# First attention: products of weights and values in eight 64-row tiles over two PSUM banks

## The chip, the cores and the metric

The kernel runs on one core of a Trainium2 chip. The metric is the device time of one execution in microseconds (us). Three runs of the kernel before took 1479.85, 1480.92 and 1483.95 us; their median is 1480.92.

The names of the engines are those of the profile: PE is TensorE (matmuls), PEld the loading of weights into TensorE (it runs beside PE), DVE is VectorE, ACT ScalarE, POOL GpSimd, and SP the engine that issues most DMAs. PSUM, where matmuls put their results, has eight banks; one bank holds a tile of 128 partitions by 512 fp32 numbers.

## The reference

The program is one layer stack over a sequence of 1024 tokens of width 512: a first attention, a feed-forward part with experts, a second attention with 4-bit weights, and the same feed-forward part again, each behind a layer norm and with a residual. The change lies in the first attention alone:

```
q = hidden_state @ wq + bq      # 32 heads of 16
k = hidden_state @ wk + bk      # 8 groups of 16, each shared by 4 heads
v = hidden_state @ wv + bv
scores = jnp.einsum('bhqd,bhkd->bhqk', q, k) * scale
probs = jax.nn.softmax(scores, axis=-1)
out = jnp.einsum('bhqk,bhkd->bhqd', probs, v)
out = jnp.swapaxes(out, -1, -2).reshape(B, -1, HEAD_DIM * NUM_HEADS)
return out @ wo + bo
```

There is no mask: each of the 32 heads weighs all 1024 keys for all 1024 queries.

## The kernel before

The first attention works on pairs of heads, 16 of them (`PAIRS`). For each pair it goes through the keys in eight tiles of 128 (`kt`, `NT` = 8). One turn of that inner loop (lines 530 to 561) is called a step here; there are 128 steps.

Queries and keys are split into a high and a low part and stacked, so that a score matmul contracts 64 rows. The stacks fill rows 0 to 63 (`low`) and 64 to 127 (`high`), with the same content, so two 64-row matmuls can run side by side, one on each half of the array. `side_by_side` (L396) takes matmuls from two lists in turn, one for each half. I call such a couple a slot. A step issues:

- Scores for a later pair, up to four or five of 128 queries by 512 keys (`half_score`, matmul L337, into a tile `sc` of a pool of three banks). DVE takes the largest of each row straight from PSUM (L346). These maxima are needed before the exponentials of that pair.
- Exponentials of the present pair (`exponentials`), four for each step, u = 0 to 3 (two heads by two halves of the queries). Each is two matmuls into one bank `st`: keys by queries (L378), and a second one that subtracts the maxima (L386). ACT then writes exp of the bank to `pT` (L390). In the high list stand u = 0, 1 and 3, in the low list u = 2 behind three scores.
- The products of the step before (`weighted(*behind)`): for each u a matmul of `v_sb` (128 keys by 32 columns: 16 values and 16 ones, which give the sum of the weights) with `pT[:, u]` into rows 32u to 32u + 31 of the one bank `po` (L411). The four column tiles share the array. These matmuls are fp32, and each shows as two records, one for each pass. The bank gathers over the eight steps of a pair.

After the last key tile DVE copies `po` to `oT` (L420). At kt = 3 of the next pair `tail` transposes `oT` on PE into a bank `pt` and DVE divides by the sums (L431 to L436). At even kt `place_largest` transposes the maxima of a later pair, if they are complete, into a bank `mp` (L360); ACT copies it (L362) and DMAs place it. Every fourth pair `project_out` multiplies by the output weights into a bank `py` (L451).

The eight PSUM banks are dealt out at lines 248 to 250: three to `sc`, four to the pool `st_ps`, one to `po`. The pool `st_ps` serves `st`, but also `mp`, `pt`, `py` and the banks of the stages ahead of and behind the loop. A tile takes a bank that has been read out; where none is free, its first matmul waits.

The order on PE in this loop is the order of the program text (`manual_schedule`, L502), so a matmul that waits holds back everything behind it on PE. The order on the other engines is set by the framework's scheduler.

Of the kernel before, what the change touches and what calls it, by code (L numbers as in the profile page):

```python
# [11 lines left out]
F32 = mybir.dt.float32  # L12
# [4 lines left out]
ALU = mybir.AluOpType  # L17
AX = mybir.AxisListType
PSUM = bass.MemoryType.PSUM

P = 128
S = 1024
C = 512
NC_ = C // P
NT = S // P
# [16 lines left out]
def kernel(  # L42
# [28 lines left out]
    nc = tc.nc  # L71

    def pool(stack, name, bufs=1, space=None):
        kw = {} if space is None else {"space": space}
        return stack.enter_context(tc.tile_pool(name=name, bufs=bufs, **kw))
# [124 lines left out]
    def attention_a():  # L200
# [6 lines left out]
        with ExitStack() as ph:  # L207
# [38 lines left out]
                nc.gpsimd.memset(m.bitcast(F32), 0.0)  # L246

            sc_ps = pool(ph, "a_sc_ps", 3, PSUM)
            st_ps = pool(ph, "a_st_ps", 4, PSUM)
            av_ps = pool(ph, "a_av_ps", 1, PSUM)  # L250

            def bank():
# [54 lines left out]
            v_sb = big.tile([P, NT, G, 32], F32, name="v_sb")  # L307
# [63 lines left out]
            pos, pTs = {}, {}  # L371
# [32 lines left out]
            def weighted(pair, kt):  # L404


                if kt == 0:
                    pos[pair] = av_ps.tile([P, C], F32, tag="po", name="po")
                po, pT = pos[pair], pTs.pop((pair, kt))
                for u in range(4):  # L410
                    nc.tensor.matmul(  # L411
                        po[ts(u, 32), :],
                        v_sb[:, kt, pair // 2, :],
                        pT[:, u],
                        start=(kt == 0),
                        stop=(kt == NT - 1),
                    )
                if kt == NT - 1:
                    oT = work.tile([P, C], F32, tag="oT", name="oT", bufs=1)
                    nc.vector.tensor_copy(oT, pos.pop(pair))  # L420
                    tails.append((pair, oT))

            tails = []
# [62 lines left out]
            low, high = slice(0, 64), slice(64, 128)  # L486
# [15 lines left out]
            with tc.manual_schedule(engines={mybir.EngineType.PE}):  # L502
# [26 lines left out]
                for pair in range(PAIRS):  # L529
                    for kt in range(NT):  # L530
# [15 lines left out]
                        if behind is not None:  # L546
                            weighted(*behind)
# [11 lines left out]
                        if kt == 1 and pair == PAIRS - 1:  # L559
                            place_ffn_weights(shared)  # L560
                            load_ffn_weights()
                weighted(*behind)
                project_out(2, 1, lambda: tail(*tails.pop()))

# [111 lines left out]
    def attention_b():  # L676
# [5 lines left out]
        with ExitStack() as ph:  # L682
# [311 lines left out]
            with tc.manual_schedule(engines={mybir.EngineType.PE}):  # L994
# [174 lines left out]
                for i, t in enumerate(todo):  # L1169
# [5 lines left out]
                    nc.sync.dma_start(out_v[:, t // 2, t % 2], x_sb[:, t // 2, t % 2])  # L1175

    attention_a()
    attention_b()

# [68 lines left out]
```

## Time and profile before

| What | Value |
|---|---|
| Median of three runs | 1480.92 us |
| The profiled execution, its own time | 1482.0 us |
| Its span, first to last instruction | 1480.2 us |
| Mean granted TensorE clock | 0.991 |
| PE busy, share of the span | 96% |
| First and last product matmul of the first attention (L411) | 78.8 to 470.1 us |
| DMA, mean | 107 GB/s |

From 80 to 440 us the stretches of 40 us show PE busy for 39.2 to 39.5 us each, DVE for 31 to 37 and ACT for 22 to 29. The time is in one profiled execution, so sums made from its rows are set against its own 1480.2 or 1482.0 us.

How to read the lines: a group line gives the source line, the engine, the operation, result and operands by the program's names, shapes and count; then busy time in us and the mean ns of one; then the idle time of that engine just before such instructions, and what ended it. `64*128` behind a matmul is the part of the array that it takes, rows by columns. A timeline line gives the start in us, the length in us, the engine, and in square brackets how long the engine had been idle and who released it; several instructions of one kind are merged, with their count behind x. The ends of matmuls are modelled, so their starts are the better measure. A fp32 matmul is two records.

### The profile page before, as it was taken

How to read it: one execution, taken by the hardware profiler on the slowest of the kernel's cores; microseconds unless marked ns; L12 is line 12 of the kernel's file. 1: busy time of each engine (PE TensorE's matmuls, PEld its weight loads, DVE VectorE, ACT ScalarE, POOL GpSimd, SP SyncE). 2: the span in 40 equal slices, each digit the busy share in tenths (PEclk: the TensorE clock that was granted, in tenths of full speed). 3: DMA queues.
4: the chain of work that ended last, by engine and by line, in shares of the span. 5: the costliest groups of instructions: out<-in, count | busy, mean ns of one | idle time of the engine just before them, and what ended most of it. 6: DMA issues, size and time to landing. Idle time of an engine off the chain costs nothing.

```text
span 1480.2 us, 21368 instructions
## 1 busy us (share of the span) xinstructions
PE 1418.6 (96%) x6967; PEld 895.0 (60%) x6967; DVE 1228.6 (83%) x2290; ACT 827.7 (56%) x1580; POOL 461.1 (31%) x365
## 2 busy tenths in 40 slices
PE   6999999999999997999999999999999999999888
PEld 4344444444444554777777777776777777777564
DVE  4799979889882677798989999998998999989783
ACT  2167657667676235665665655655665565665420
POOL 4200000000000425536536446445445545433120
PEclk9999999999999999999999999999999999999999
DMA  4352314233330425555555555555555555555511
GB/s 126 57 105 48 65 34 74 41 54 56 58 112 2 126 71 127 124 138 144 141 139 140 142 134 146 143 127 142 146 131 135 126 142 144 119 131 148 143 45 57
DMA packets 135870, 158.47 MB, mean 107 GB/s; under 512 B 34912, under 2 KB 111392, under 8 KB 135504
## 3 DMA queue, kind: packets, MB, share of 16 engines
q1 hardware_dynamic: 135340, 156.49, 44.3%
q8 instruction: 56, 0.92, 0.3%
q0 software_dynamic: 352, 0.59, 0.1%
q14 instruction: 54, 0.44, 0.1%
q10 hardware_dynamic: 68, 0.03, 0.0%
HBM read 33.03 MB, written 6.05 MB: 26 GB/s over the span
## 4 chain that ended last, share of the span: by engine, by line
PE 68%; DVE 15%; DMA 6%; SPq 2%; POOL 2%; ACT 2%; issue 2%; DVEq 0%; ACTq 0%; POOLq 0%
PE pc L948 12%; PE sc L872 12%; PE po L411 7%; PE sc L337 7%; DVE m L346 6%; PE pp L801 4%; DMA xT<-blocks 4%; PE pp L802 4%; PE bank L610 3%; PE py L801 3%; PE py L802 3%; PE st L378 2%; DVE shared L982 2%; SPq L911 2%; PE py L451 2%
## 5 line engine op out<-in xcount | busy, mean ns | idle before, releaser
L346 DVE TENSOR_REDUCE m<-sc 128x1 f32<-128x512 f32 x512 | 319.8, 682 | 25.7 <-PE st L378 20.3
L390 ACT ACTIVATE pT<-st 128x512 f32<-128x512 f32 x512 | 264.7, 602 | 128.5 <-PE st L386 109.5
L872 PE MATMUL sc<-kT,qT 128*128 128x512 f32 (+3 forms) x768 | 291.5, 489 | 4.5 <-ACT x_sb L883 2.5
L888 ACT ACTIVATE x_sb<-x_sb,total 128x768 f32<-128x768 f32 (+7 forms) x256 | 196.4, 774 | 138.8 <-DVE total L887 138.8
L883 ACT ACTIVATE x_sb<-sc,m 128x768 f32<-128x768 f32 (+7 forms) x256 | 188.2, 735 | 133.4 <-DVE m L877 128.5
L948 PE MATMUL pc<-xT,v_sb 128*128 128x256 f32 (+1 forms) x1024 | 242.1, 363 | 17.7 <-DMA xT<-blocks 17.7
L877 DVE TENSOR_REDUCE m<-sc 128x1 f32<-128x768 f32 (+7 forms) x256 | 191.9, 750 | 44.0 <-PE sc L875 42.4
L948 PEld LDWEIGHTS pc<-xT,v_sb 128*128 128x128 f32 x1024 | 191.6, 191 | 53.1 <-issue 17.6
L337 PE MATMUL sc<-ks,qs 64*128 64x512 f32 x512 | 186.5, 448 | 5.4 <-DVE m L346 2.7
L872 PEld LDWEIGHTS sc<-kT,qT 128*128 128x128 f32 x768 | 138.7, 192 | 75.6 <-issue 63.7
L386 PE MATMUL st<-ms_q,ones 64*128 64x512 f32 x512 | 177.9, 413 | 0.7 <-DMA ms_q<-mT 0.7
L378 PE MATMUL st<-qs,ks 64*128 64x512 f32 x512 | 175.9, 422 | 1.4
L982 DVE SCALAR_TENSOR_TENSOR shared<-py,o_sc,shared 128x512 f32<-128x512 f32 x248 | 173.8, 729 | 2.9 <-PE py L802 2.9
L900 DVE STREAM_TRANSPOSE blocks<-x_sb 128x128 f32<-128x128 f32 (+3 forms) x192 | 156.6, 816 | 20.4 <-ACT x_sb L888 14.1
L337 PEld LDWEIGHTS sc<-ks,qs 64*128 64x128 f32 x512 | 83.8, 184 | 146.3 <-DVE m L346 129.6
L801 PE MATMUL pp<-x_hl,w 128*128 128x512 f32 x384 | 166.4, 433 | 2.7 <-DVE shared L982 1.5
L709 POOL TENSOR_SCALAR w<-r 128x512 fp32r<-128x512 int32 x80 | 119.7, 1497 | 135.7 <-PE pp L802 78.8
L802 PE MATMUL pp<-x_hl,w 128*128 128x512 f32 x384 | 152.1, 396 | 2.4 <-DVE x_hl L759 2.4
L827 POOL TENSOR_TENSOR qT<-acc,cos_sb 128x512 f32<-128x512 f32 x62 | 79.5, 1283 | 226.0 <-DVE acc L815 211.3
L815 DVE SCALAR_TENSOR_TENSOR acc<-pp,q_sc,acc 128x512 f32<-128x512 f32 x192 | 140.9, 734 | 7.9 <-ACT acc L813 5.9
L411 PE MATMUL po<-pT,v_sb 128*32 128x512 f32 x1024 | 136.6, 604 | 0.0
L828 POOL TENSOR_TENSOR turned<-turned,sin_sb 128x512 f32<-128x512 f32 x78 | 100.5, 1288 | 55.4 <-DMA turned<-acc 54.2
(173 smaller groups left out, 1940.3 us busy)
## 6 DMA issues: line engine op xcount, KB each, us to landing
xT<-blocks SPq DMA_DIRECT2D x128, 240.0 KB, 4.3
xT<-blocks SPq DMA_DIRECT2D x128, 176.0 KB, 3.5
turned<-acc SPq DMA_DIRECT2D x160, 128.0 KB, 2.6
pT<-x_sb SPq DMA_DIRECT2D x128, 112.0 KB, 2.5
qs<-q_hl SPq DMA_DIRECT2D x128, 64.0 KB, 2.4
qs<-shared SPq DMA_DIRECT2D x128, 64.0 KB, 2.5
r<-in_qwq_dram SPq DMA_DIRECT2D x32, 256.0 KB, 2.8
r<-in_qwo_dram SPq DMA_DIRECT2D x32, 256.0 KB, 2.8
```

Of the source, the lines that this page charges most:

```text
L337: nc.tensor.matmul(sc, qs[pair % NS][rows, jj, ts(t, P)], ks[pair // 2 % NS][rows, ts(half, C)], start=True, stop=True,)
L346: nc.vector.tensor_reduce(ms[pair][:, at : at + 1], sc, AX.X, ALU.max, negate=True)
L378: nc.tensor.matmul(st, ks[pair // 2 % NS][rows, ts(kt, P)], qs[pair % NS][rows, u // 2, ts(u % 2, C)], start=True, stop=False,)
L390: nc.scalar.activation(pTs[pair, kt][:, u], st, AF.Exp, scale=DA**-0.5)
L411: nc.tensor.matmul(po[ts(u, 32), :], v_sb[:, kt, pair // 2, :], pT[:, u], start=(kt == 0), stop=(kt == NT - 1),)
L801: nc.tensor.matmul(ps, lhsT, high, start=True, stop=False)
L802: nc.tensor.matmul(ps, lhsT, low, start=False, stop=True)
L872: nc.tensor.matmul(sc[:, k0:k1], qT[:, ts(t, P)], kT[:, k0:k1], start=True, stop=(k1 < keys))
L877: nc.vector.tensor_reduce(m, sc[:, :keys], AX.X, ALU.max, negate=True)
L888: nc.scalar.activation(p, p, AF.Copy, scale=total)
L948: nc.tensor.matmul(pc[:, 2 * P * i + lo : 2 * P * (i + 1)], v_sb[:, k, ts(g, DB)], some, start=(k == 0), stop=(k == 2 * pair + 1),)
L982: nc.vector.scalar_tensor_tensor(y, py, scale, y, ALU.mult, ALU.add)
```

## The change

`st_ps` gets three banks in place of four. The bank gained goes to the products: a pair has two tiles `po0` and `po1` in place of one `po`. Each of the four matmuls of a step becomes two: one contracts rows 0 to 63 of the keys (`low`) into `po0`, the other rows 64 to 127 (`high`) into `po1`. A step so issues eight matmuls of 64 rows and 32 columns where it issued four of 128 rows and 32 columns. At the end of a pair ACT copies `po0` to `oT`, and DVE adds `po1` to it; before, one copy on DVE did it.

```diff
-            st_ps = pool(ph, "a_st_ps", 4, PSUM)
+            st_ps = pool(ph, "a_st_ps", 3, PSUM)
             av_ps = pool(ph, "a_av_ps", 1, PSUM)
...
                 if kt == 0:
-                    pos[pair] = av_ps.tile([P, C], F32, tag="po", name="po")
-                po, pT = pos[pair], pTs.pop((pair, kt))
+                    pos[pair] = [
+                        av_ps.tile([P, C], F32, tag=f"po{i}", name=f"po{i}") for i in range(2)
+                    ]
+                pT = pTs.pop((pair, kt))
                 for u in range(4):
-                    nc.tensor.matmul(
-                        po[ts(u, 32), :],
-                        v_sb[:, kt, pair // 2, :],
-                        pT[:, u],
-                        start=(kt == 0),
-                        stop=(kt == NT - 1),
-                    )
+                    for po, rows in zip(pos[pair], (low, high)):
+                        nc.tensor.matmul(
+                            po[ts(u, 32), :],
+                            v_sb[rows, kt, pair // 2, :],
+                            pT[rows, u],
+                            start=(kt == 0),
+                            stop=(kt == NT - 1),
+                        )
                 if kt == NT - 1:
                     oT = work.tile([P, C], F32, tag="oT", name="oT", bufs=1)
-                    nc.vector.tensor_copy(oT, pos.pop(pair))
+                    first, second = pos.pop(pair)
+                    nc.scalar.copy(oT, first)
+                    nc.vector.tensor_tensor(oT, oT, second, ALU.add)
                     tails.append((pair, oT))
```

## The prediction

> **What bounds the kernel now.** I read the page first: TensorE (PE) is busy all the way, and the product line of the first attention (L411) carries 7% of the chain that ended last.
>
> ```profile
> PE 1418.6 (96%) x6967; PEld 895.0 (60%) x6967; DVE 1228.6 (83%) x2290; ACT 827.7 (56%) x1580; POOL 461.1 (31%) x365
> ...
> L346 DVE TENSOR_REDUCE m<-sc 128x1 f32<-128x512 f32 x512 | 319.8, 682 | 25.7 <-PE st L378 20.3
> L390 ACT ACTIVATE pT<-st 128x512 f32<-128x512 f32 x512 | 264.7, 602 | 128.5 <-PE st L386 109.5
> ...
> L411 PE MATMUL po<-pT,v_sb 128*32 128x512 f32 x1024 | 136.6, 604 | 0.0
> ```
>
> The 1024 records of L411 are 128 groups of eight: four column tiles, two fp32 passes each. By the answer for line L411 they start from 78.8 to 470.1 us, so a step (one pair of heads, one tile of 128 keys) lasts 391.3/128 = 3.06 us on average. Next I asked the timeline of PE for one plain step:
>
> ```profile
> 206.44 0.50 PE L337 MATMUL sc<-ks,qs 64*128 64x512 f32 x1
> 206.44 0.50 PE L378 MATMUL st<-qs,ks 64*128 64x512 f32 x1
> 206.78 0.39 PE L337 MATMUL sc<-ks,qs 64*128 64x512 f32 x1
> 206.79 0.39 PE L386 MATMUL st<-ms_q,ones 64*128 64x512 f32 x1
> ...
> 207.49 0.39 PE L378 MATMUL st<-qs,ks 64*128 64x512 f32 x1
> 207.73 0.50 PE L337 MATMUL sc<-ks,qs 64*128 64x512 f32 x1
> 207.73 0.50 PE L386 MATMUL st<-ms_q,ones 64*128 64x512 f32 x1
> 208.16 1.06 PE L411 MATMUL po<-pT,v_sb 128*32 128x512 f32 x8
> 209.16 0.50 PE L337 MATMUL sc<-ks,qs 64*128 64x512 f32 x1
> ```
>
> Six slots of two 64-row matmuls side by side (1.72 us), then the group (1.00 us), then the next step: 2.72 us; most steps read 2.70. In 2.70 us DVE needs four reductions, which follow each other every 0.60 us: 2.40. ACT needs four exponentials, 2.06 us from the first start to the last end. So PE sets these steps. The starts of the product groups over one pair give eight intervals: 2.70, 2.71, 3.75, 2.71, 3.28, 2.70, 2.71, 2.99. The 3.75 is the step with the transposes of `tail`, the 3.28 the one with `place_largest`, the 2.99 the one where DVE also copies oT. The 3.75 matters most:
>
> ```profile
> 212.79 0.39 PE L386 MATMUL st<-ms_q,ones 64*128 64x512 f32 x1
> ...
> 213.25 0.62 PE L386 MATMUL st<-ms_q,ones 64*128 64x512 f32 x2
> 213.96 0.49 PE L378 MATMUL st<-qs,ks 64*128 64x512 f32 x1
> 213.96 0.50 PE L337 MATMUL sc<-ks,qs 64*128 64x512 f32 x1
> 214.29 0.39 PE L386 MATMUL st<-ms_q,ones 64*128 64x512 f32 x1
> 214.62 0.64 PE L411 MATMUL po<-pT,v_sb 128*32 128x512 f32 x4
> ```
>
> ```profile
> 213.96 0.18 PEld L378 LDWEIGHTS st<-qs,ks 64*128 64x128 f32 x1 [0.52 <-ACT pT L390]
> ```
>
> ```profile
> 213.31 2.06 ACT L390 ACTIVATE pT<-st 128x512 f32<-128x512 f32 x4 [1.22 <-PE st L386]
> ```
>
> Here `pt` holds one of the four st buffers, so the four exponentials e0 to e3 have three. The first half of e3 (L378) waits until ACT has read e0: 213.31 + 0.60 = 213.91, and it starts at 213.96. From the first slot (212.45, same answer) to the group that is 2.17 us; in the plain step 1.72. **One st buffer short costs 0.45 us.** This is the situation that the change makes permanent.
>
> **The change part by part.**
>
> *st_ps from 4 to 3.* Every step now has three st buffers for four exponentials. e3's first matmul asks in the fifth slot, 1.05 us after the step's start (207.49). e0 is read 0.52 us after its second matmul (206.79 to 207.31 in ACT's timeline) and 0.60 us long, so it is free at 207.95. Queued behind the waiting load on PE, in program order, are the fourth score, the second half of e3 and the product group, so the whole step moves by 0.45. DVE and ACT wait with it, and both have room. What is late next is again PE. Nothing else could lend a buffer: the other two hold e1 and e2, whose exponentials come later.
>
> *The products.* Eight matmuls of 64 rows and 32 columns in place of four of 128 rows: 2048 records in place of 1024, 16 loads per group in place of 8. The streams are as long as before (512 columns, fp32, two passes), so if all eight tiles run side by side the group keeps its length. No row shows a 64*32 tile. The nearest are the four column tiles of L411, which start 7 ns apart, and the 64-row pairs of L337 and L378, which share a slot. Four more tiles at 7 ns are +0.03 us per group. The Trainium skill, "TensorE: Matmul & The Clock Gate", section "Measured speedup vs the span model", gives about 4 ns per further tile: +0.016, or 2 us over 128 groups against 4 by the row; I take the row. The bounds: none, and a second turn of both passes (in the timeline one group starts at 205.45 and its second four matmuls at 205.90, so a pass of the group lasts about 0.45; as streams, 2 × 0.43), so up to +0.85 per group, 109 us.
>
> *The turn-over between tile shapes.* Now the group pays to enter (214.29 to 214.62 is 0.33, a slot in mid-step 0.23: 0.10), to leave (a group of 1.00 against two streams of 0.43, the distance at which the fp32 passes of L451 follow each other: 0.14) and for the first slot after it (206.44 to 206.78 is 0.34: 0.11), together about 0.35. If 64*128 to 64*32 needs no turn-over, since the row halves stay, up to 0.3 is saved. No row here shows that pair. The Trainium skill, "TensorEngine Tiling (Array Packing)", section "Key Properties", says that a change of tiling mode, not just of tile, drains TensorE, and 64×128 and 64×32 are different modes in its list. By the rule nothing is saved; by the hopeful reading 0.3 × 128 = 38 us. I take nothing: the row that exists, 64-row to 128*32, also changes columns and pays.
>
> *Evacuation.* DVE's copy of oT (681 ns, 16 times) becomes a copy on ACT (about 0.60, the length of L390) and an add on DVE of the copy's length. DVE gains nothing. ACT is idle 1.12 us between the fourth exponential of a step and the first of the next, just when the group ends, so the copy fits. The add follows, some 0.75 to 1.5 us into the step; the next pair's first group, which needs both banks, comes at 2.17. I cost this at nothing; were that cover gone, at most 0.6 × 15 = 9 us. Behind the DVE add are the reductions, which have 0.8 us of room per step in the longer step.
>
> *The special steps.* Tail: with pt on one of three buffers, e2 waits for e0 as well (213.96 in place of 213.25), with the second half of e1 behind it, and e3 then waits for pt's last reading by DVE (about 214.75) or for e1 (about 215.1): +0.84 to +1.17, I take 1.0. place_largest: the fourth score there waits for DVE anyway until 219.91, which hides most of the 0.45; +0.16 with the tile starts. The 2.99 step has DVE as its bound; the new PE length 3.19 takes over: +0.25, with some allowance.
>
> *The sum per pair.* Five plain steps from 2.70 to 3.19 (2.72 + 0.45 + 0.03, rounded): 5 × 0.48 = 2.42; plus 1.0 + 0.16 + 0.25 = 3.83. Thirteen middle pairs: 50. Pair 0 has three steps of 3.30 with extra scores, where DVE hides most: 2. The last scores end in pair 14; its later steps and pair 15's last 2.58, where nothing hides the wait (e3's second half then also loses the overlap of its load): to 3.18, +0.6 each, 8.3 for both pairs. Sum 60 us. The other users of st (projections, values, layer norm) keep three buffers against evictions of 0.7 us and matmul groups of 1.7 us: nothing. The second attention and both feed-forward parts are untouched.
>
> Against its own run the profiled execution (span 1480.2, 1482.0 us in all) would go to 1540 and 1542. The median of the runs, 1.1 us lower, goes to **1541**.
>
> **The rivals.**
>
> *The turn-over goes away* (1503). 60 − 38 = +22. For it: all matmuls of a step then have 64 rows. Against: the rule above, and the columns still change. Partly so: 1490 to 1530.
>
> *The eight tiles do not run side by side, so the change does not do what it says* (about 1645). The group takes its passes twice: +109 on top of 56 us of waits. For it: twice the loads and instructions in the queue at once. Against: the two row halves share slots today, and four column tiles share a pass. In part, 1560 to 1645.
>
> *The group falls to the pace of its neighbours* (about 1447, faster). One mechanism in the product group: a half-height pass is two further slots of 0.23 with its load hidden, so the group's share of the step falls from 1.20 (1.00 + 0.10 + 0.10) to 0.50: −0.70 × 128 = −90, against +56 for the waits. It decides once the share is below about 0.73. For it: 64-row matmuls here take 0.23 per pass. Against: those are fp32r, and the fp32 rows stream two passes of 0.43.
>
> **How the numbers follow.** The wait as costed with the turn-over kept: 0.64 (1525 to 1556, for the tail step and the tile start). Turn-over partly or wholly gone: 0.20. Not side by side, wholly or in part: 0.11. At the neighbours' pace: 0.05, of which a little ends at no change. A measurement of this kernel tells about 0.3% (4.4 us) from nothing. Faster 0.04, same 0.03, slower 0.93. Range 1500 to 1580: it leaves out the faster end, the lowest part of the second case and most of the third, some 0.2 together.
>
> **What the changed profile would show.** Waits of L378's loads on L390 in nearly every step, 0.5 us each, some 60 us in all where there are now 14.8 (23 times). Plain steps of 3.19 us, tail steps of 4.7. L411 with 2048 records in groups of about 1.03 us: 1.9 would be the second rival, below 0.7 the third. A group that enters 0.23 after the last slot, with the next second slot 0.23 on, would mean no turn-over. I am wrong on the main step if L378 does not wait for ACT in plain steps.

## The result and the profile after

The changed kernel takes 1541.8 us (median of 4 runs, 1538.98 to 1544.82) against 1480.73 us for the kernel before on the same chip. The ratio is 1.0402, with a 95% interval of 1.0386 to 1.0417. The forecast was 1541, in a range of 1500 to 1580. Ratios and their intervals leave out a run that took over 1.5% more than the fastest of its kernel; this concerns one run of st2_whole alone.

The profiled execution has a span of 1539.4 us in place of 1480.2. From the first to the last start of a product matmul it was 391.4 us and is now 448.4: +57.0 of the +59.2 lie in the 128 steps. The stretch ahead of them grew by 1.2 us, what follows by 0.9.

The page of the changed kernel, first the busy times, then the two groups that answer to the ones shown of before (`weighted` now stands at L415):

```profile
PE 1458.6 (95%) x7991; PEld 903.4 (59%) x7991; DVE 1231.6 (80%) x2290; ACT 840.0 (55%) x1596; POOL 460.9 (30%) x365
...
L378 PEld LDWEIGHTS st<-qs,ks 64*128 64x128 f32 x512 | 91.7, 185 | 95.8 <-ACT pT L390 78.5
...
L415 PE MATMUL po<-pT,v_sb 64*32 64x512 f32 x2048 | 140.0, 605 | 0.0
```

The loads of L378 now wait for ACT for 78.5 us; in the kernel before it was 14.8. L415 has twice the records of L411, and its busy time is up by 3.4 us only (136.6 before): the records of a group overlap almost wholly.

The timeline of PE for a plain step of the changed kernel:

```profile
228.12 0.49 PE L337 MATMUL sc<-ks,qs 64*128 64x512 f32 x1
228.12 0.49 PE L378 MATMUL st<-qs,ks 64*128 64x512 f32 x1
228.46 0.39 PE L337 MATMUL sc<-ks,qs 64*128 64x512 f32 x1
228.46 0.39 PE L386 MATMUL st<-ms_q,ones 64*128 64x512 f32 x1
...
229.63 0.49 PE L378 MATMUL st<-qs,ks 64*128 64x512 f32 x1
229.63 0.50 PE L337 MATMUL sc<-ks,qs 64*128 64x512 f32 x1
229.96 0.39 PE L386 MATMUL st<-ms_q,ones 64*128 64x512 f32 x1
230.29 1.09 PE L415 MATMUL po<-pT,v_sb 64*32 64x512 f32 x16
231.31 0.33 PE L437 MATMUL pt<-ident,oT 128*128 128x128 f32 x1
```

And the load that waits in it, from the timeline of weight loads, with the exponentials of that step from ACT's:

```profile
229.63 0.18 PEld L378 LDWEIGHTS st<-qs,ks 64*128 64x128 f32 x1 [0.51 <-ACT pT L390]
```

```profile
228.98 2.06 ACT L390 ACTIVATE pT<-st 128x512 f32<-128x512 f32 x4 [1.04 <-PE st L386]
```

This is the tail step of the kernel before, in a step whose four exponentials meet no `pt` (the transposes at 231.31 come behind them). The first exponential starts at 228.98 and is 0.60 us long; 0.05 us later, at 229.63, the fourth exponential's first matmul starts. From the step's start to the group it is 2.17 us, as it was in that tail step, in place of 1.72. The group takes 1.02 us (230.29 to 231.31) in place of 1.00.

In all 157 waits of L378 on ACT from 80 to 530 us sum to 88.6 us (the first and third of these lines from the view of waits: for loads, and for matmuls where the load was done):

```profile
PEld st L378 <- ACT pT L390: 78.1, 133, 1.0
PEld sc L337 <- DVE m L346: 73.3, 97, 1.7
...
PE st L378 <- ACT pT L390: 10.5, 24, 0.6
...
PE st L378 <- DVE o_sb L442: 3.3, 15, 0.5
```

These waits grew by 73.8 us, the loop by 57.0. That fits the second line, which was 117.0 us in 200 waits before: where DVE already set the pace of a step, the new wait in part takes the place of an old one. (A load can be idle while PE still works, so such sums only show the direction.)

### The profile page after: what moved, and what is told of

Same layout as the page of the kernel before. It is cut to its first block, busy times and chain, and to the rows that moved or that the text cites. A ratio compares the mean times of both kernels' runs of the same rounds, so it can differ in the third digit from the quotient of the medians.

```text
span 1539.4 us, 23463 instructions
## 1 busy us (share of the span) xinstructions
PE 1458.6 (95%) x7991; PEld 903.4 (59%) x7991; DVE 1231.6 (80%) x2290; ACT 840.0 (55%) x1596; POOL 460.9 (30%) x365
## 4 chain that ended last, share of the span: by engine, by line
PE 68%; DVE 11%; DMA 7%; ACT 6%; issue 3%; SPq 3%; POOL 3%; ACTq 0%; DVEq 0%; POOLq 0%
PE pc L954 11%; PE sc L878 11%; PE po L415 9%; PE sc L337 6%; PE st L378 5%; PE pp L807 4%; ACT pT L390 4%; DMA xT<-blocks 4%; PE pp L808 4%; PE bank L616 3%; PE py L807 3%; DMA turned<-acc 3%; PE st L386 2%; PE py L808 2%; SPq L917 2%
## 5 line engine op out<-in xcount | busy, mean ns | idle before, releaser
L390 ACT ACTIVATE pT<-st 128x512 f32<-128x512 f32 x512 | 268.3, 602 | 168.1 <-PE st L386 163.1
L378 PE MATMUL st<-qs,ks 64*128 64x512 f32 x512 | 209.8, 452 | 21.9 <-ACT pT L390 10.5
L378 PEld LDWEIGHTS st<-qs,ks 64*128 64x128 f32 x512 | 91.7, 185 | 95.8 <-ACT pT L390 78.5
L415 PE MATMUL po<-pT,v_sb 64*32 64x512 f32 x2048 | 140.0, 605 | 0.0
```

Of the source, the lines that this page charges most:

```text
L378: nc.tensor.matmul(st, ks[pair // 2 % NS][rows, ts(kt, P)], qs[pair % NS][rows, u // 2, ts(u % 2, C)], start=True, stop=False,)
L390: nc.scalar.activation(pTs[pair, kt][:, u], st, AF.Exp, scale=DA**-0.5)
L415: nc.tensor.matmul(po[ts(u, 32), :], v_sb[rows, kt, pair // 2, :], pT[rows, u], start=(kt == 0), stop=(kt == NT - 1),)
```

## The experiments

My theory: the fourth bank of `st_ps` was what let the fourth exponential of a step start before ACT had read the first; nearly all of the loss is that wait. The rivals: the eight tiles themselves cost the time (loads, instructions, the turn-over between tile shapes), or the new way of evacuating on ACT and DVE does.

All rows of this table are intervals between starts of product groups in one middle pair (the seventh), in us, read from each kernel's trace. The loop is the time from the first to the last start of a product matmul. The third interval holds the tail (the second, where the tail goes first), the fifth `place_largest`, the eighth the evacuation.

| Kernel | 1 | 2 | 3 | 4 | 5 | 6 | 7 | 8 | sum |
|---|---|---|---|---|---|---|---|---|---|
| before | 2.70 | 2.71 | 3.75 | 2.71 | 3.28 | 2.70 | 2.71 | 2.99 | 23.55 |
| after | 3.19 | 3.19 | 4.67 | 3.18 | 3.45 | 3.20 | 3.19 | 3.19 | 27.26 |
| st3_whole | 3.16 | 3.17 | 4.65 | 3.16 | 3.43 | 3.16 | 3.18 | 3.17 | 27.08 |
| parity_st3 | 3.16 | 3.17 | 4.65 | 3.16 | 3.43 | 3.16 | 3.18 | 3.17 | 27.08 |
| sc2_whole | 3.40 | 3.41 | 4.16 | 3.40 | 3.67 | 3.40 | 3.40 | 3.60 | 28.44 |
| sc2_halves | 3.42 | 3.43 | 4.18 | 3.43 | 3.69 | 3.41 | 3.43 | 3.92 | 28.91 |
| tail_first | 2.71 | 3.30 | 2.71 | 2.71 | 3.28 | 2.70 | 2.70 | 2.99 | 23.10 |
| tail_first_act | 2.71 | 3.29 | 2.71 | 2.71 | 3.28 | 2.71 | 2.70 | 2.70 | 22.81 |
| tail_first_halves | 3.19 | 3.78 | 3.19 | 3.19 | 3.45 | 3.19 | 3.19 | 3.19 | 26.37 |

**st3_whole: the bank alone.** The kernel before, with one line changed; one bank stays unused.

```diff
-            st_ps = pool(ph, "a_st_ps", 4, PSUM)
+            st_ps = pool(ph, "a_st_ps", 3, PSUM)
```

> The kernel before with three st banks and one bank left unused; the products stay four tiles of 128 rows. If the missing st bank is the cause: nearly all of the loss, 1538 us (+57), plain steps of 3.16 us, tail steps of 4.65. If the eight tiles of 64 rows are the cause (loads, turn-over, queue): 1481 to 1490. If the evacuation over ACT and DVE is: 1481 to 1490 as well.

Measured: 1536.26 us against 1482.55 for before, run beside it, ratio 1.0364 (1.0351 to 1.0378). The loop takes 444.4 us, 53.0 of the 57.0 us that the change added. A plain step of it in the timeline of PE, with the four tiles of 128 rows:

```profile
222.11 0.39 PE L386 MATMUL st<-ms_q,ones 64*128 64x512 f32 x1
...
222.57 0.61 PE L386 MATMUL st<-ms_q,ones 64*128 64x512 f32 x2
223.28 0.50 PE L378 MATMUL st<-qs,ks 64*128 64x512 f32 x1
223.28 0.50 PE L337 MATMUL sc<-ks,qs 64*128 64x512 f32 x1
223.62 0.40 PE L386 MATMUL st<-ms_q,ones 64*128 64x512 f32 x1
223.95 0.64 PE L411 MATMUL po<-pT,v_sb 128*32 128x512 f32 x4
```

```profile
223.28 0.18 PEld L378 LDWEIGHTS st<-qs,ks 64*128 64x128 f32 x1 [0.52 <-ACT pT L390]
```

From 222.57 to 223.28 it is 0.71 us; the plain step of the kernel before has 0.24 there (207.25 to 207.49). The second view names the wait, and no 64-row product is near. The eight tiles cannot be its cause.

**parity_st3: the evacuation.** Three st banks, the old tiles of 128 rows, and two product banks filled in turn by even and odd key tiles, evacuated by the same two instructions as in the changed kernel (against the kernel before, shortened):

```diff
+                po, pT = pos[pair][kt % 2], pTs.pop((pair, kt))
...
-                        start=(kt == 0),
-                        stop=(kt == NT - 1),
+                        start=(kt < 2),
+                        stop=(kt >= NT - 2),
...
+                    nc.scalar.copy(oT, first)
+                    nc.vector.tensor_tensor(oT, oT, second, ALU.add)
```

> Three st banks, products of 128 rows as before, but even key tiles go to po0 and odd ones to po1, evacuated as in the changed kernel: a copy on ACT, an add on DVE. Bank theory: as st3_whole, 1538, at most 2 more for the evacuation, so that what is left to the changed kernel (3 to 4 us) belongs to the tile shape. If the evacuation costs its length on the path: 9 us more than st3_whole (0.6 us by 15).

Measured: 1537.64 us, ratio 1.0372 (1.0359 to 1.0386); its loop takes 444.7 us against 444.4 of st3_whole, and the row of the table is the same in every step. The evacuation is hidden here, but this is the easier case: `po0` is complete one step earlier, and its copy starts 2.0 us ahead of the last group. For the changed kernel the table itself answers: there the copy starts 1.18 us behind the start of the last group and the add ends at 2.84, yet the interval is 3.19, as in the plain steps. It is hidden there too, with 0.35 us left before the next group writes the banks. What the changed kernel has beyond parity_st3 is left to the tile shape: 3.186 in place of 3.166 us, means of 40 plain steps each, so 0.02 us.

**sc2_whole and sc2_halves: the eight tiles with four st banks.** The kernel has eight banks to deal out, so four for st and two for products need one from the scores. The first kernel is a control (before, with two score banks), the second has the change's products on top.

```diff
-            sc_ps = pool(ph, "a_sc_ps", 3, PSUM)
-            st_ps = pool(ph, "a_st_ps", 3, PSUM)
+            sc_ps = pool(ph, "a_sc_ps", 2, PSUM)
+            st_ps = pool(ph, "a_st_ps", 4, PSUM)
```

> A control: the kernel before with two score banks in place of three, and four st banks. The third score of a step then waits for the first reduction (1.28 us after the step's start in place of 0.58), so a plain step should last about 3.4 us and the whole about 1560 (1545 to 1580). Its use is as a base for the next kernel.

> The changed kernel with four st banks and two score banks: the eight 64-row tiles without the loss of an st bank. Against sc2_whole, bank theory: +3 us (0.02 to 0.03 us by 128 groups, and nothing for the evacuation), 0 to +5. If the eight tiles were the cause: +50 to +60. If they saved the turn-over: -20 to -38.

Measured: 1565.36 us, ratio 1.0572 (1.0546 to 1.0599), for the control, and 1580.84, ratio 1.0663 (1.0641 to 1.0684), for the halves. The control came as costed, with plain steps of 3.40. The difference of the two, 15 us, is not: 3 was expected, at most 5. The loops take 462.4 and 468.6 us, so +6.2. In the pair of the table the halves take 0.47 us more: 0.32 of it in the eighth interval, 3.92 in place of 3.60, and 0.02 in each of the others, as expected of the tiles. There the add stands between two reductions, in DVE's timeline:

```profile
202.86 0.69 DVE L346 TENSOR_REDUCE m<-sc 128x1 f32<-128x512 f32 x1 [0.75 <-PE st L378]
203.47 0.68 DVE L426 TENSOR_TENSOR oT<-oT,po 128x512 f32<-128x512 f32 x1
204.06 1.97 DVE L346 TENSOR_REDUCE m<-sc 128x1 f32<-128x512 f32 x3
```

With two score banks PE waits for each reduction in turn, so a DVE instruction of 0.6 us in that place is on the path; in the changed kernel, with three, it was not. The evacuation is free only with that cover.

The other 9 us between the medians go with the clock of the runs. At a mean granted clock of 0.992 the control took 1563.48 us and the halves 1569.85; at 0.990 it was 1566.83 and 1572.74, at 0.979 and 0.978 1577.84 and 1583.88. So at like clock the two lie some 6 us apart, as their loops do. But four of the six runs with the halves had a clock of 0.985 or less, and only one of the control. Why the halves met the lower clock more often is open; only one execution of each was profiled.

One place in these two traces is clean: the last pair has no scores left, so neither score banks nor DVE matter, and four st banks are there. Its plain steps last 2.58 to 2.60 us in the control and 2.60 to 2.61 with the eight tiles. The tiles cost 0.02 us per group, and save nothing.

**st2_whole: the dose.** The kernel before with two st banks.

> The dose: the kernel before with two st banks (two left unused). If the banks are dealt as I read it, the third exponential of a step waits for the first (1.51 us after the step's start) and the fourth for the second (2.68), the group starts at 3.34 and a plain step lasts about 4.35 us, 1.2 more than with three. Whole: about 1690 (1670 to 1730, tail steps uncertain). If the loss with three banks came from something that one bank does once, the second bank would cost about the same again: 1592.

Measured: 1726.11 us, ratio 1.162 (1.158 to 1.166). Plain steps at full clock:

```profile
641.34 0.50 PE L378 MATMUL st<-qs,ks 64*128 64x512 f32 x1 [0.55 <-ACT pT L390]
641.34 0.73 PE L386 MATMUL st<-ms_q,ones 64*128 64x512 f32 x2
642.53 0.50 PE L378 MATMUL st<-qs,ks 64*128 64x512 f32 x1 [0.46 <-ACT pT L390]
642.53 0.49 PE L337 MATMUL sc<-ks,qs 64*128 64x512 f32 x1
642.86 0.39 PE L386 MATMUL st<-ms_q,ones 64*128 64x512 f32 x1
643.19 1.07 PE L411 MATMUL po<-pT,v_sb 128*32 128x512 f32 x8
```

The step starts at 639.82; the third exponential starts 1.52 us later, the fourth 2.71, the group 3.37, and the next step at 644.18: 4.36 us. Expected were 1.51, 2.68, 3.34 and 4.35. The second bank costs 1.2 us per plain step where the first cost 0.46, as the order of reads says and not as a fixed price for one bank would. The whole time lies in the expected range, but 36 us above its middle. The profiled run, at 1764.97 us the longest of the four, had a lower granted clock in parts of the loop, which is told below. Its middle pairs at full clock take 36.6 to 36.7 us, those mostly at the lower one 48.0 to 48.3. The other three runs took 1718.72 to 1732.73 us, with mean clocks of 0.956 to 0.971; the kernel before, run beside them, had 0.990 to 0.994.

**tail_first, tail_first_act and tail_first_halves: the same wait taken away.** The kernel before had one step per pair with this wait. In tail_first the transposes go ahead of the products, so DVE can read `pt` while PE is busy with the group.

```diff
+                        if kt == 3:
+                            for item in tails:
+                                tail(*item)
+                            tails.clear()
                         if behind is not None:
                             weighted(*behind)
                         behind = pair, kt
-                        if kt == 3:
-                            for item in tails:
-                                tail(*item)
-                            tails.clear()
```

> The kernel before, four st banks, with the transposes of the tail put ahead of the product group of that step in place of behind it, so that DVE reads pt while PE does the products. Bank theory: the fourth exponential of the next step finds its bank read out, the tail step falls from 3.75 to 3.30, -0.45 by 15 = -6.7 us, 1476. If the 0.45 belongs to the transposes themselves (turn-over of the array) and not to the bank: no change, 1482.

Measured: 1476.07 us, ratio 0.9952 (0.9937 to 0.9966). Two pieces of the PE timeline around a tail:

```profile
154.94 0.66 PE L431 MATMUL pt<-ident,oT 128*128 128x128 f32 x4
155.53 1.07 PE L411 MATMUL po<-pT,v_sb 128*32 128x512 f32 x8
```

```profile
156.53 0.50 PE L378 MATMUL st<-qs,ks 64*128 64x512 f32 x1
...
157.33 0.62 PE L378 MATMUL st<-qs,ks 64*128 64x512 f32 x2
157.56 0.38 PE L386 MATMUL st<-ms_q,ones 64*128 64x512 f32 x1
157.80 0.50 PE L337 MATMUL sc<-ks,qs 64*128 64x512 f32 x1
157.81 0.50 PE L386 MATMUL st<-ms_q,ones 64*128 64x512 f32 x1
158.24 0.64 PE L411 MATMUL po<-pT,v_sb 128*32 128x512 f32 x4
```

The transposes still take their 0.59 us (154.94 to 155.53), so that is their own price. The step behind them has its slots in a row: from its first slot to the group it is 1.71 us, as in a plain step (1.72), where it was 2.17. The 0.45 us belonged to the bank.

In tail_first_act ACT does the copy of `oT` as well.

```diff
-                    nc.vector.tensor_copy(oT, pos.pop(pair))
+                    nc.scalar.copy(oT, pos.pop(pair))
```

> As tail_first, and the copy of oT on ACT in place of DVE. The step with that copy is bound by DVE (2.99 in place of 2.70), and ACT has an idle gap of 1.1 us there: -0.29 by 15 = -4.3 us more, about 1471.5. If ACT's copy delays the exponentials behind it: no gain over tail_first, or a loss of up to 0.6 by 15.

Measured: 1469.93 us, ratio 0.9913 (0.9899 to 0.9928): faster than both kernels of this case, and its interval lies below that of tail_first. The eighth interval fell from 2.99 to 2.70, the length of a plain step. Its copy, from the view of the tile oT (least, median and largest length in ns, first and last start in us):

```profile
L420 ACT COPY oT<-po x16: 586/587/618, 101.3 to 459.3; 128x512 f32<-128x512 f32 x16
```

tail_first_halves makes the same move of the tail in the changed kernel.

> The changed kernel, three st banks, with the tail ahead of the products. The tail step loses the waits that pt adds on top (4.67 to 3.19 + 0.58 = 3.77): -0.9 by 15 = -13 us, 1528; the plain steps stay at 3.19. If the bank were not the cause: 1542, as the changed kernel.

Measured: 1528.63 us, ratio 1.0301 (1.0282 to 1.0319). The tail step fell from 4.67 to 3.78, the plain steps stayed at 3.19. The gain is 13 us, but about half of it is no part of the loss: the kernel before had the wait of 0.45 us in its tail step too, and gained 6.9 us by the same move. With the tail ahead of the products in both, the change costs 52.6 us (1528.63 against 1476.07) in place of 61.1. So the waits that `pt` adds in the tail step were a seventh of the loss at most, and nearly all of the rest is the wait that the missing bank brings to every step.

## Why the prediction was right

- **The bank.** The price of 0.45 us was read from one step of the kernel before and carried to all. It held: 3.19 us were forecast for a plain step and 3.18 to 3.20 measured, and st3_whole shows that the bank alone does it. Two slips in the working change nothing: 207.31 + 0.60 is 207.91, and the 207.95 takes in most of the 0.05 us between the end of an exponential and the next matmul into its bank; and 5 × 0.48 is 2.40, not 2.42.
- **Eight tiles.** +0.03 us per group was forecast from the 7 ns between tiles, +0.02 measured. All eight ran side by side; that rival fell. So did the one with the pace of the neighbours: the group takes 1.02 us, two fp32 passes as before, though its rows are halved (the second half of its records starts 0.46 us behind the first, 227.10 to 227.56).
- **The turn-over.** I took it as kept, by the Trainium skill, "TensorEngine Tiling (Array Packing)", section "Key Properties". The trace agrees: from the last slot to the group it is 0.33 us (229.96 to 230.29), and in st3_whole, with tiles of 128 rows, 0.33 as well (223.62 to 223.95). From the first slot to the second it is 0.34 in both (228.12 to 228.46, 221.77 to 222.11). Keeping 64 rows while the columns change saves nothing here.
- **The evacuation.** Costed at nothing, and the eighth interval of the changed kernel, 3.19, shows nothing. The cover that I named, room on DVE, is real: with two score banks it is gone and each pair pays 0.3 us. The add starts 1.14 us into the step, within the 0.75 to 1.5 that I had put.
- **The special steps.** Tail +1.0 forecast, +0.92 measured in the middle pairs, but +0.48 in the last (3.44 to 3.92); place_largest +0.16 and +0.17; the step with the evacuation +0.25 and +0.20; the steps without scores +0.6 and +0.57. The path of the tail step was right as well: fifteen times, the number of tails in the loop, L378 waited for DVE's last reading of `pt` (L442 in the view of waits above). A middle pair so grew by 3.71 us, not 3.83, but the two in which the output projection falls twice (pairs 4 and 8, counted from 0) by 2.91 only, which the forecast had not set apart. The thirteen middle pairs grew by 46.6 us, where 50 were put.
- **Mis-sized.** Pair 0 was put at +2 and grew by 3.3: its first step took 4.72 us, since the granted clock was 0.83 from 80 to 90 us in that execution. With the same products and banks tail_first_halves has 3.35 there, so it is not the change's. And the waits of L378's loads on ACT came to 78.1 us in 133 waits, not some 60 at 0.5 each.

The sum of 60 us for the loop stands against 57.0 measured in the profiled execution, of which some 1.4 are the first step at the lower clock. Another 2.1 us lie outside the loop, where nothing was put: 0.9 behind it and 1.2 ahead. The kernels with `po0` and `po1` and three st banks have their first product at 79.8 to 80.0 us, before and st3_whole at 78.8; why is open. So the mechanism was right, but that 1541 comes within 1 us of the measured 1541.8 is luck: misses of some microseconds, up and down, cancel.

## What to carry to other kernels

A buffer pool is worth what the consumer's latency is worth at the moment when the next writer asks: write the times of one step beside each other (asked at, free at), and look in the trace for a step where one buffer is already held by something else, since it shows the price of having one less. Ask also how many banks a rearrangement takes from its neighbours before asking what it saves; here the saving did not exist, and what was left of the change was the bank that it took. And a step that already pays such a wait can be relieved for nothing by issuing the holder of the buffer ahead of a long group of other work.

## What I had not expected of the hardware

In the kernel with two short waits in each step, TensorE's granted clock fell in parts of the loop. In st2_whole a step at full clock lasts 4.36 us and in it PE waits twice for about half a microsecond; yet whole runs of steps last 6.50 us in its profiled run, the longest of four. In the stretches 124 to 129 and 130 to 170 us of that kernel (busy times of PE, PEld, DVE, ACT and POOL, then the granted clock, the share of DMA and GB/s):

```profile
124.00:129.00 5.00, 3.99 (x30) 1.24 (x22) 2.81 (x5) 2.62 (x5) 0.00 (x0) 1.00 0.34 56
130.00:170.00 40.00, 34.87 (x128) 12.43 (x128) 18.77 (x35) 14.33 (x27) 0.00 (x0) 0.58 0.22 38
```

In the second stretch consecutive slots stand 0.43 us apart in place of 0.23. With three banks and one wait of half a microsecond per 3.19 us the clock stood at 1.00 from 90 to 528 us. In sc2_whole too, where PE waits for the reductions and is busy for 85% of the time, it was 1.00 from 100 to 540 us. In st2_whole PE is busy for 78% at full clock.

The lower clock is not an accident of one run: all four of st2_whole had a mean clock of 0.932 to 0.971, against 0.990 to 0.994 of the kernel before beside them. That the waits cause it is argued from this, not shown. The waits alone do not settle when it falls, since the same kind of steps kept a clock of 1.00 there from 258 to 398 us. What sets the limit was not tried. What is shown is that this kernel lost more than its waits.
